# A graph network layer on one core: one-hot of the sums moved within the step, loads moved between queues, bias rows made on ScalarE

## The chip, the core and the metric

The kernel runs on one core of a Trainium2 chip. Time is device time in microseconds (us) of one launch. Each kernel is run several times, and runs of two kernels are compared on the same chip. The core's engines work side by side, each through its own instruction order: TensorE (PE in the profile, its weight loads PEld), VectorE (DVE), ScalarE (ACT), GpSimd (POOL) and SyncE (SP, which here only issues transfers and reads addresses). An instruction waits for semaphores of other engines and of transfers; everything behind it on its engine waits too.

## The reference

A node has 128 features, there are N = 12500 nodes and E = 400000 edges, sorted by target (`dst`). Per edge a message is built from both ends' rows, scaled by an edge weight and by a small network over 32 edge features; scores go through a softmax over all edges of the same target; values are summed per target.

```python
h = jnp.maximum(_layernorm(x, axis=-1), 0.0)
message = (h @ w_src + b_src)[src] + (h @ w_dst)[dst]
message = message * edge_weight1 * _radial_mlp(edge_attr_32, ...)
message = message @ w_sep + b_sep
msg_h = message.reshape(n_edges, H, AH + VH)
alpha = _smooth_leaky_relu(msg_h[:, :, :AH])
value = msg_h[:, :, AH:]
score = jnp.einsum('ehk,ahk->eh', alpha, alpha_dot)
att = _segment_softmax(score, dst, n_nodes)[..., None]
out = jax.ops.segment_sum(value * att, dst, num_segments=n_nodes)
x = x + out.reshape(n_nodes, H * VH) @ w_proj + b_proj
```

Everything is float32; H = 8 heads with 16 + 16 channels.

## The kernel before

All stages are written in an order fixed by hand: within a stage the program's order is each engine's order. Tiles come from pools with a fixed number of buffers, and a tile that is made anew waits until the readers of its older buffer are done.

**The node stage** (lines 154 to 342) makes two tables in device memory, `t_src` and `t_dst`, from layer norm, relu and two products. It goes over 98 tiles of 128 nodes in 25 quads of 4 tiles. `stats` (DVE) and `norm` (ACT) run ahead, `turn` transposes a quad on PE and copies it on DVE, `products(i)` multiplies, copies to `ms` (4 buffers, mostly by ACT) and has SP store `ms` to the two tables. SP's queue holds, in this order: the 8 loads of x (L162, L163); the targets as `cur` and, shifted by one edge, as `prev`, both 125 rows of 3200 words (L169 to L172); the first target of each section, `base` (L176, two times 400 single words); the sections' ends, `ends` (L177, 1600 single words); 14 loads of weights in block form (L188 to L194); and then the table stores. ACT's queue starts with two loads and 15 more through `load` (L110). `fits()` after quad 12 checks that the targets are sorted and every section spans less than 64 targets. `cuts()` after the last quad turns `prev` and `cur` into marks (`sm`), stored to `same` for the softmax, and makes small constants (`w_s`, `v_out`, `b_s`, `far`, `tgt`).

**The step loop** (`windows`, L656 to L1181) does 400 steps, each for 1000 edges in two sections of 500. `step(k)` carries several steps at once: POOL's gathers of source rows for k+4 and k+5 (8 indirect transfers per step, L739), the edge network for k+1 to k+3, the message and scores of k, and for c = k - 12 the values times softmax weights (`values`, into `pvx`) and their sum per target (`sums`, L912: a product of `pvx` with a one-hot `oh` of each edge's place in its window of 64 targets). Every 8 steps the softmax of 16 sections runs: a scan forward (L852), a scan backward and a subtraction (L857, L862), an exponential on ACT and a transposition. In every eighth step from step 47 on, 25 times, `add_x` adds the output bias to a block of x that `load_x` fetched two steps before.

DVE's order in a regular step is: the one-hot's two instructions (L888, L891), `rad` twice, `mT` twice, `pvx` of section 0, `mr`, `al` of section 0, `pvx` of section 1, `al` of section 1, `ohT`, `m`, and behind these a scan where one is due. PE's order is `p3`, the sources' transposition, the message, V of section 0, pa, the network's first layer, V of section 1, sources, pa, second layer, `sums`, a transposition and, in odd steps, the scores.

After the last k 14 more steps empty the pipeline, with jobs between them that combine the windows' edges (L1144 to L1181).

**The last stage** (L1213 to L1289) divides the sums by the weights' total (`quotients`, 12 tiles at a time), transposes (`turn`), multiplies by `w_proj` and adds x and the value bias. Its loads are `g` (SP, 12 tiles each, 9 of them, three ahead) and `x_fin` (ACT's queue, 8 loads). Per tile DVE adds `v_out` times a factor per node (`has`) to x (L1270), and per quad it adds the product (L1274); SP stores the output.

Of the kernel before, what the change touches and what calls it, by code (L numbers as in the profile page):

```python
# [56 lines left out]
def gnn_kernel(ctx: ExitStack, tc: tile.TileContext, a: dict, out: bass.AP):  # L57
# [47 lines left out]
    ident = const.tile([P, P], F32, name="ident")  # L105
    make_identity(nc, ident)

    def load(name, shape, ap=None, eng=None):
        t = const.tile(shape, F32, name="c_" + name)
        (eng or nc.scalar).dma_start(out=t, in_=a[name] if ap is None else ap)  # L110
        return t

    eps = const.tile([P, 1], F32, name="eps")
    nc.vector.memset(eps, LN_EPS)
    ones = const.tile([P, P], F32, name="ones")
# [38 lines left out]
    with tc.tile_pool(name="node", bufs=2) as np_, tc.tile_pool(name="node1", bufs=1) as n1, \  # L154
# [6 lines left out]
        for t0, t1 in groups:  # L161
            nc.sync.dma_start(out=x_all[:, t0:t1, :], in_=x_v[:, t0:t1, :])  # L162
        nc.sync.dma_start(out=x_all[:tail, NF, :], in_=x[NF * P:, :])  # L163
        dst_r = dst.rearrange("(p c) -> p c", p=RP)
        cur = n1.tile([RP, RC], I32, name="cur")
        prev = n1.tile([RP, RC], I32, name="prev")
        ends = n1.tile([100, 8, 2], I32, name="ends")
        eb = n1.tile([P, NS, 2], I32, name="eb")
        nc.sync.dma_start(out=cur, in_=dst_r)  # L169
        nc.vector.memset(prev[0:1, 0:1], -1)  # L170
        nc.sync.dma_start(out=prev[0:1, 1:RC], in_=dst_r[0:1, 0:RC - 1])
        nc.sync.dma_start(out=prev[1:RP, :], in_=dst[RC - 1:E - 1].rearrange("(p c) -> p c", c=RC))  # L172
        at = dst[0:1]
        with nc.allow_non_contiguous_dma(reason="the sections' ends"):
            for f in range(2):
                nc.sync.dma_start(out=base[:, f, :], in_=dst_h[f:f + 1, :, 0])  # L176
            nc.sync.dma_start(out=ends, in_=bass.AP(  # L177
                at.tensor, at.offset, [[8 * SEC, 100], [SEC, 8], [SEC - 1, 2]]))

        w1b = const.tile([P, P], F32, name="w1b")  # L180
        nc.vector.memset(w1b, 0.0)
        w2b = const.tile([P, P], F32, name="w2b")
        w3b = const.tile([P, C], F32, name="w3b")
        b12 = const.tile([P, 2], F32, name="b12")
        for f in range(2):
            for q in range(2):
                o = (2 * q + f) * RAD
                nc.sync.dma_start(out=w1b[o:o + RAD, f * FC:(f + 1) * FC], in_=a["fc_w1"])  # L188
            s = slice(f * FC, (f + 1) * FC)
            for q in range(2):  # L190
                nc.sync.dma_start(out=w2b[s, q * FC:(q + 1) * FC], in_=a["fc_w2"])
            nc.sync.dma_start(out=w3b[s, :], in_=a["fc_w3"])
            nc.sync.dma_start(out=b12[s, 0:1], in_=a["fc_b1"])
            nc.sync.dma_start(out=b12[s, 1:2], in_=a["fc_b2"])  # L194
        b_n = load("b_n", [C, 1], a["b_src"].rearrange("o c -> c o"))
        dot = load("dot", [C, 1])
        heads = load("heads", [C, C])
        w1, b1 = load("fc_w1", [RAD, FC]), load("fc_b1", [FC, 1])
        w2, b2 = load("fc_w2", [FC, FC]), load("fc_b2", [FC, 1])
        w3, b3 = load("fc_w3", [FC, C]), load("fc_b3", [C, 1])  # L200
        w_a, b_a = load("w_a", [C, C]), load("b_a", [C, 1])
        w_v = load("w_v", [C, C])
        w_proj = load("w_proj", [C, C])
        b_out = load("b_out", [P, C], a["b_proj"].to_broadcast([P, C]))
        b_v = load("b_v", [C, 1])


        mv = n1.tile([P, NB, 2], F32, name="mv")
# [60 lines left out]


        def fits():
            gt = n1.tile([RP, RC], BF16, name="gt")
            nc.vector.tensor_tensor(gt, prev, cur, op=ALU.is_gt)
            cnt = n1.tile([P, 2], F32, name="cnt")
            nc.vector.memset(cnt, 0.0)
            nc.vector.tensor_reduce(cnt[:RP, 0:1], gt, AX.X, ALU.add)
            span = n1.tile([100, 8], F32, name="span")
            nc.vector.tensor_sub(span, ends[:, :, 1], ends[:, :, 0])
            nc.vector.tensor_scalar(span, span, float(W - 1), None, op0=ALU.is_ge)
            nc.vector.tensor_reduce(cnt[:100, 1:2], span, AX.X, ALU.add)  # L280
            tot = nps.tile([1, 1], F32, name="tot", bufs=1)
            for j in range(2):
                nc.tensor.matmul(tot, cnt[:, j:j + 1], ones[:, 0:1], start=(j == 0), stop=(j == 1))
            nc.vector.tensor_copy(bad, tot)
            nc.sync.dma_start(out=ends_d[:, 1:2 * NS + 1].rearrange("o (p c) -> (o p) c", p=100),
                              in_=ends.rearrange("p s i -> p (s i)"))
            none = n1.tile([1, 2], I32, name="none")
            nc.vector.memset(none, -1)
# [12 lines left out]
        v_out = const.tile([P, C], F32, name="v_out")  # L301

        def cuts():
            sm = n1.tile([RP, RC], BF16, name="sm")
            nc.vector.tensor_tensor(sm, prev, cur, op=ALU.not_equal)
            nc.vector.tensor_scalar(sm, sm, RESTART, None, op0=ALU.mult)
            nc.sync.dma_start(out=same[:, 0:E].rearrange("o (p c) -> (o p) c", p=RP), in_=sm)
# [24 lines left out]
        for i in range(Q):  # L332
            if i % 2 == 0 and 4 * i + G < NB:
                stats(4 * i + G, min(4 * i + 2 * G, NB))
            if i + 2 < Q:
                norm(i + 2)
            if i + 1 < Q:
                turn(i + 1)
            products(i)
            if i == 12:  # L340
                fits()
        cuts()


    chunks = [(t, min(CH, TPI - t)) for t in range(0, TPI, CH)]
# [310 lines left out]
    def windows():  # L656
# [5 lines left out]
        with tc.tile_pool(name="wk2", bufs=2) as sp, tc.tile_pool(name="ps", bufs=1, space=PSUM) as pp, \  # L662
# [214 lines left out]
                nc.scalar.copy(Pem[m].rearrange("p t q h -> p t (q h)"), pt)  # L877


            def sums_begin(c):  # L880
                pvx[c] = sp.tile([T, 2, TS, ROW], F32, name="pvx")
                q = c % MP * 2
                for f in range(2):
                    nc.scalar.copy(pvx[c][:, f, :, C:ROW], Pem[c // MP][:, :, q + f, :])
                _, loc = prep[c // 16]
                ohs[c] = sp.tile([T, 8, W], F32, name="oh")
                t0 = c % 16 * 8
# [60 lines left out]
            def step(k):  # L948
# [28 lines left out]
                if has(k + 1):  # L977
                    split_md(k + 1, 0)
                if has(c):
                    sums_begin(c)  # L980
                rad = mlp3(k) if has(k) else None
                if has(k):
                    sources(k, 1)
# [13 lines left out]
                    mlp1(k + 2)  # L997
                if has(c):
                    values(c, 1)

                if has(k + 1):
                    sources(k + 1, 0)
# [210 lines left out]
    with tc.tile_pool(name="fin", bufs=3) as fp, tc.tile_pool(name="fin1", bufs=1) as f1, \  # L1213
# [4 lines left out]
        for t0, t1 in groups:  # L1218
            nc.scalar.dma_start(out=x_all[:, t0:t1, :], in_=xb_v[:, t0:t1, :])
        nc.scalar.dma_start(out=x_all[:tail, NF, :], in_=xb[NF * P:N, :])  # L1220
        gs, qs, qTs, has = {}, {}, {}, {}
        XQ = 12
        starts = list(range(0, NB, XQ))
# [35 lines left out]

        def finish(i):  # L1260
            t0, t1 = quads[i]
            qT = qTs.pop(i)
            py = fps.tile([P, 4, C], F32, name="py")
            for t in range(t0, t1):
                n = rows(t)
                nc.tensor.matmul(py[:n, t - t0, :], qT[:, t - t0, :n], w_proj, start=True, stop=True)
            for t in range(t0, t1):
                n, u = rows(t), t % XQ
                xt = x_all[:n, t, :]
                nc.vector.scalar_tensor_tensor(xt, v_out[:n], has[t0 // XQ][:n, u:u + 1], xt,  # L1270
                                               op0=ALU.mult, op1=ALU.add)
            for n, u0, u1 in blocks(t0, t1):
                y = x_all[:n, u0:u1, :]
                nc.vector.tensor_add(y, py[:n, u0 - t0:u1 - t0, :], y)  # L1274
                nc.sync.dma_start(out=out_v[:, u0:u1, :] if n == P else out[NF * P:N, :].unsqueeze(1), in_=y)

        NG = len(starts)
        for i in range(3):
            load_g(i)
        quotients(0)  # L1280
        turn(0)
# [44 lines left out]
```

## Time and profile before

| what | value |
|---|---|
| median of 3 runs | 4723.23 us (4720.04 to 4723.61) |
| the profiled execution: its time | 4712.63 us |
| its span | 4710.8 us |
| mean granted TensorE clock | 0.964 |
| node stage, to the first load of the step stage | 155.0 us |
| POOL's first gather | 160.28 us |
| first load of the last stage | 4626.5 us |

Busy over the whole span, and the two stages at the ends as 40 slices show them (one digit is a slice of 117.8 us in tenths of busy time; PEclk is the granted clock):

```profile
PE 4212.0 (89%) x29692; PEld 2344.1 (50%) x29692; DVE 3081.2 (65%) x6005; ACT 1921.9 (41%) x4595; POOL 3136.0 (67%) x3223
...
PE   4669998999999999999999999999999999999974
...
PEclk8779999999999999999999999999999999999987
```

A line of the profile's tables reads: line of the kernel, engine, operation, output <- inputs, shapes, count, busy time and mean of one, then the engine's idle time just before and what ended most of it. In a timeline the first two numbers are start and duration in us. A wait list reads: who waited for whom, total us, how often, longest. An engine's share over the whole span is a mean over stages with different limits, so the stages are read on their own.

### The profile page before, as it was taken

The numbers are of one execution on the slowest core, as the hardware profiler recorded it, in microseconds if no ns is written. First come the engines' busy times: TensorE is split into PE (matmuls) and PEld (weight loads), VectorE is DVE, ScalarE is ACT, GpSimd is POOL, SyncE is SP. The second block draws the span as 40 slices with busy tenths as digits, with TensorE's granted clock in tenths as the row PEclk, the third lists the DMA queues.
The fourth block names the chain that finished last, engine by engine and source line by source line (L and its number), as shares of the span: only waits on it lengthen the run. The fifth ranks groups of instructions, "written<-read, shape, count | busy, mean of one in ns | idle before, by whom it ended". The sixth has DMA issues, their size and how long they took to land.

```text
span 4710.8 us, 88096 instructions
## 1 busy us (share of the span) xinstructions
PE 4212.0 (89%) x29692; PEld 2344.1 (50%) x29692; DVE 3081.2 (65%) x6005; ACT 1921.9 (41%) x4595; POOL 3136.0 (67%) x3223
## 2 busy tenths in 40 slices
PE   4669998999999999999999999999999999999974
PEld 3325554554555555555545555555555555555553
DVE  4436665766766666666666666666666666666666
ACT  3324443443443444443433444444444444444421
POOL 0467776776777777777766777777777767777601
PEclk8779999999999999999999999999999999999987
DMA  4667767777776777777777777777677777777724
GB/s 160 168 162 173 175 167 172 174 178 175 170 176 171 169 176 175 172 178 174 170 175 170 177 174 169 179 172 164 171 174 169 171 168 170 172 168 174 173 64 173
DMA packets 901312, 796.36 MB, mean 169 GB/s; under 512 B 530125, under 2 KB 776829, under 8 KB 900598
## 3 DMA queue, kind: packets, MB, share of 16 engines
q1 hardware_dynamic: 794830, 573.36, 46.8%
q0 software_dynamic: 102816, 210.37, 21.5%
q10 hardware_dynamic: 3202, 6.92, 0.4%
q8 instruction: 234, 3.83, 0.4%
q14 instruction: 230, 1.88, 0.1%
HBM read 649.99 MB, written 140.67 MB: 168 GB/s over the span
## 4 chain that ended last, share of the span: by engine, by line
PE 66%; DVE 10%; DMA 9%; SPq 6%; ACT 5%; issue 4%; POOL 1%; ACTq 0%; POOLq 0%; DVEq 0%
PE pa L820 14%; PE V L901 13%; PE misc L912 7%; PE p L790 6%; PE pm L803 6%; PE pm L811 4%; PE p L758 4%; PE misc L831 4%; PE p L773 4%; DMA md<-t_dst 2%; DMA sc_d<-Sp 2%; PE m L749 2%; ACT sl L822 2%; DMA agg<-ob 2%; DVE al L824 2%
## 5 line engine op out<-in xcount | busy, mean ns | idle before, releaser
L739 POOL DMA_INDIRECT gs<-t_src,idx x3200 | 3121.6, 976 | 1347.2 <-issue 800.8
L822 ACT ACTIVATE sl<-pa,c_b_a 128x500 f32<-128x500 f32 x800 | 541.4, 677 | 1595.5 <-PE pa L820 1594.7
L824 DVE SCALAR_TENSOR_TENSOR al<-pa,sl 128x500 f32<-128x500 f32 x800 | 543.1, 679 | 828.8 <-ACT sl L822 723.6
L820 PE MATMUL pa<-mT,c_w_a 128*128 128x500 f32 x1600 | 851.2, 614 | 244.2 <-DVE mT L816 173.3
L901 PE MATMUL V<-c_w_v,mT 128*125 128x128 f32 x6208 | 895.5, 288 | 0.3
L901 PEld LDWEIGHTS V<-c_w_v,mT 128*125 128x125 f32 x6208 | 746.4, 190 | 290.7 <-issue 176.8
L794 DVE SCALAR_TENSOR_TENSOR rad<-p,c_fc_b,w_b 128x500 f32<-128x500 f32 x800 | 552.9, 733 | 307.2 <-PE p L790 305.7
L903 DVE TENSOR_TENSOR pvx<-V,Pem 125x512 f32<-125x512 f32 x776 | 531.9, 685 | 114.4 <-PE V L901 107.8
L816 DVE SCALAR_TENSOR_TENSOR mT<-pm,c_b_n,rad 128x500 f32<-128x500 f32 x800 | 552.5, 733 | 6.5 <-PE pm L811 6.5
L803 PEld LDWEIGHTS pm<-ident,gs 125*128 125x128 f32 x3200 | 356.7, 142 | 312.8 <-issue 292.3
L803 PE MATMUL pm<-ident,gs 125*128 125x125 f32 x3200 | 505.0, 280 | 7.9 <-DMA gs<-t_src,idx 7.9
L912 PE MATMUL misc<-pvx,oh 125*64 125x136 f32 x6400 | 470.1, 288 | 31.4 <-DVE pvx L903 27.6
L912 PEld LDWEIGHTS misc<-pvx,oh 125*64 125x64 f32 x6400 | 364.5, 138 | 182.9 <-issue 178.6
L790 PE MATMUL p<-h,w3b 64*128 64x500 f32 x1600 | 446.0, 634 | 2.4 <-ACT h L776 2.4
L820 PEld LDWEIGHTS pa<-mT,c_w_a 128*128 128x128 f32 x1600 | 245.0, 193 | 284.5 <-DVE mT L816 195.4
L811 PE MATMUL pm<-ohT,m 64*128 64x500 bf16 x2400 | 323.9, 376 | 0.0
L758 PE MATMUL p<-eT,w1b 64*128 64x250 f32 x1600 | 287.5, 437 | 1.0 <-ACT eT L751 1.0
L725 ACT CAST m<-md 128x128 bf16<-128x128 f32 x400 | 118.3, 296 | 401.1 <-DMA md<-t_dst 400.8
L758 PEld LDWEIGHTS p<-eT,w1b 64*128 64x128 f32 x1600 | 124.7, 191 | 307.5 <-issue 276.3
L761 ACT ACTIVATE h<-p,b 128x500 f32<-128x500 f32 x400 | 272.4, 681 | 4.8 <-PE p L758 4.8
L776 ACT ACTIVATE h<-p,b 128x500 f32<-128x500 f32 x400 | 269.2, 673 | 3.6 <-PE p L773 3.6
L888 DVE TENSOR_TENSOR oh<-lane,loc 125x504 f32<-125x504 f32 x400 | 269.2, 673 | 0.0
(145 smaller groups left out, 3286.1 us busy)
## 6 DMA issues: line engine op xcount, KB each, us to landing
w_b<-in_edge_weight SPq DMA_DIRECT2D x400, 500.0 KB
d_b<-in_dst SPq DMA_DIRECT2D x400, 250.0 KB
gs<-t_src,idx POOLq DMA_INDIRECT x3200
e_t<-in_edge_attr SPq DMA_DIRECT2D x400, 125.0 KB
sc_d<-Sp SPq DMA_DIRECT2D x200, 250.0 KB
win<-ob SPq DMA_DIRECT2D x400, 68.0 KB
agg<-ob SPq DMA_DIRECT2D x800, 33.5 KB
md<-t_dst SPq DMA_DIRECT2D x800, 32.0 KB
```

What stands on the lines that cost most here:

```text
L739: nc.gpsimd.indirect_dma_start(out=gs[:, j, :], out_offset=None, in_=t_src[:, :], in_offset=bass.IndirectOffsetOnAxis(ap=idx[:, t:t + 1], ...
L758: nc.tensor.matmul(p1[:, q, 0:2 * T], w1b[s, :], eTs[k][s, :], start=True, stop=True)
L790: nc.tensor.matmul(p3[:, f, 0:SEC], w3b[s, :], h2s[k][s, :], start=True, stop=True)
L794: nc.vector.scalar_tensor_tensor(rad[:, s], p3[:, f, 0:SEC], b3, w_g[k][:, s], op0=ALU.add, op1=ALU.mult)
L803: nc.tensor.matmul(pms[k, f][:, t * T:(t + 1) * T], gs[:T, t, :], ident[:T, :T], start=(t == 0), stop=False, is_transpose=True, skip_group ...
L816: nc.vector.scalar_tensor_tensor(mTs[k][:, s], pm[f], b_n, rad[:, s], op0=ALU.add, op1=ALU.mult)
L820: nc.tensor.matmul(pa, w_a, mTs[k][:, f * SEC:(f + 1) * SEC], start=True, stop=True)
L822: nc.scalar.activation(sl, pa, AF.Silu, bias=b_a, scale=1.0)
L824: nc.vector.scalar_tensor_tensor(al, pa, 0.25, sl, op0=ALU.mult, op1=ALU.add)
L901: nc.tensor.matmul(V[:, t, :], mTs[c][:, o:o + T], w_v, start=True, stop=True)
L903: nc.vector.tensor_mul(pvx[c][:, f, :, 0:C].rearrange("p t (h k) -> p t h k", h=H), V.rearrange("p t (h k) -> p t h k", h=H), Pem[c // MP] ...
L912: nc.tensor.matmul(acc[f * W:(f + 1) * W, :], ohs[c][:, f * TS + t, :], pvx[c][:, f, t, :], start=(t == 0), stop=(t == TS - 1), skip_group ...
```

## The change

Four edits.

1. The one-hot of the sums: `sums_begin` is split. Its copies stay where they were (`weights`), its two DVE instructions (`one_hot`) are called after `values(c, 1)`, that is behind the second `pvx` and ahead of the second `al`. In the steps after the last k, too, they follow the two `pvx`.
2. Targets: one tile `cur` of 128 rows with 3126 words takes the place of `cur` and `prev`: 3125 words per row by one load, and the word before them by a second load of 127 single words. `fits` and `cuts` compare the tile with itself shifted by one. The marks leave as 128 rows of 3125.
3. Loads: the targets' loads and all weights (15 that were on ACT's queue, 14 that were on SP's) go to SP's queue behind the table stores of quads 0 and 1. `cuts` is called after quad 20 instead of after the last.
4. The last stage: x is loaded through SP's queue, behind the first load of `g` and ahead of the second. `v_out` times `has` is made by ACT into a new tile `vh`, four instructions per quad; GpSimd adds `vh` to x, one instruction per quad (two for the last); DVE adds the product.

```diff
+        def load_targets():
+            nc.sync.dma_start(out=cur[:, 1:CC + 1], in_=dst.rearrange("(p c) -> p c", p=P))
+            at = dst[CC - 1:CC]
...
+                nc.sync.dma_start(out=cur[1:P, 0:1], in_=bass.AP(at.tensor, at.offset, [[CC, P - 1], [1, 1]]))
...
+            if i == 1:
+                load_targets()
+                load_weights()
             if i == 12:
                 fits()
-        cuts()
+            if i == 20:
+                cuts()
...
-            def sums_begin(c):
+            def weights(c):
                 pvx[c] = sp.tile([T, 2, TS, ROW], F32, name="pvx")
...
+            def one_hot(c):
                 _, loc = prep[c // 16]
...
                 if has(c):
-                    sums_begin(c)
+                    weights(c)
...
                 if has(c):
                     values(c, 1)
+                    one_hot(c)
...
+        def load_x():
+            for t0, t1 in groups:
+                nc.sync.dma_start(out=x_all[:, t0:t1, :], in_=xb_v[:, t0:t1, :])
...
         def finish(i):
             t0, t1 = quads[i]
+            vh = fp.tile([P, 4, C], F32, name="vh")
+            for t in range(t0, t1):
+                n, u = rows(t), t % XQ
+                nc.scalar.activation(vh[:n, t - t0, :], v_out[:n], AF.Identity, scale=has[t0 // XQ][:n, u:u + 1])
+            for n, u0, u1 in blocks(t0, t1):
+                y = x_all[:n, u0:u1, :]
+                nc.gpsimd.tensor_tensor(y, y, vh[:n, u0 - t0:u1 - t0, :], op=ALU.add)
...
-                nc.vector.scalar_tensor_tensor(xt, v_out[:n], has[t0 // XQ][:n, u:u + 1], xt,
-                                               op0=ALU.mult, op1=ALU.add)
...
         NG = len(starts)
-        for i in range(3):
+        load_g(0)
+        load_x()
+        for i in range(1, 3):
             load_g(i)
```

More of the change, by code (lines that the diff above doesn't have):

```diff
@@ L106, in gnn_kernel @@
     make_identity(nc, ident)
[L108 to L111, printed above, removed]
     eps = const.tile([P, 1], F32, name="eps")
@@ L163, in gnn_kernel @@
         nc.sync.dma_start(out=x_all[:tail, NF, :], in_=x[NF * P:, :])
[L164 to L178, printed above, removed]
         w1b = const.tile([P, P], F32, name="w1b")
@@ L184, in gnn_kernel @@
         b12 = const.tile([P, 2], F32, name="b12")
[L185 to L204, printed above, removed]
@@ L205, in gnn_kernel @@
-        b_v = load("b_v", [C, 1])
+        CC = E // P
+        cur = n1.tile([P, CC + 1], I32, name="cur")
+        nc.vector.memset(cur[0:1, 0:1], -1)
+        ends = n1.tile([100, 8, 2], I32, name="ends")
+        eb = n1.tile([P, NS, 2], I32, name="eb")
+        wt = {name: const.tile(shape, F32, name="c_" + name) for name, shape in (
+            ("b_src", [C, 1]), ("dot", [C, 1]), ("heads", [C, C]), ("fc_w1", [RAD, FC]), ("fc_b1", [FC, 1]),
+            ("fc_w2", [FC, FC]), ("fc_b2", [FC, 1]), ("fc_w3", [FC, C]), ("fc_b3", [C, 1]), ("w_a", [C, C]),
+            ("b_a", [C, 1]), ("w_v", [C, C]), ("w_proj", [C, C]), ("b_proj", [P, C]), ("b_v", [C, 1]))}
@@ new lines, in gnn_kernel @@
+        b_n, dot, heads, w1, b1, w2, b2, w3, b3, w_a, b_a, w_v, w_proj, b_out, b_v = wt.values()
+        def load_targets():
+            nc.sync.dma_start(out=cur[:, 1:CC + 1], in_=dst.rearrange("(p c) -> p c", p=P))
+            at = dst[CC - 1:CC]
+            with nc.allow_non_contiguous_dma(reason="single targets"):
+                nc.sync.dma_start(out=cur[1:P, 0:1], in_=bass.AP(at.tensor, at.offset, [[CC, P - 1], [1, 1]]))
+                for f in range(2):
+                    nc.sync.dma_start(out=base[:, f, :], in_=dst_h[f:f + 1, :, 0])
+                at = dst[0:1]
+                nc.sync.dma_start(out=ends, in_=bass.AP(
+                    at.tensor, at.offset, [[8 * SEC, 100], [SEC, 8], [SEC - 1, 2]]))
@@ new lines, in load_weights @@
+        def load_weights():
+            for name, t in wt.items():
+                ap = a[name]
+                if name == "b_src":
+                    ap = ap.rearrange("o c -> c o")
+                elif name == "b_proj":
+                    ap = ap.to_broadcast([P, C])
+                nc.sync.dma_start(out=t, in_=ap)
+            for f in range(2):
+                for q in range(2):
+                    o = (2 * q + f) * RAD
+                    nc.sync.dma_start(out=w1b[o:o + RAD, f * FC:(f + 1) * FC], in_=a["fc_w1"])
+                s = slice(f * FC, (f + 1) * FC)
+                for q in range(2):
+                    nc.sync.dma_start(out=w2b[s, q * FC:(q + 1) * FC], in_=a["fc_w2"])
+                nc.sync.dma_start(out=w3b[s, :], in_=a["fc_w3"])
+                nc.sync.dma_start(out=b12[s, 0:1], in_=a["fc_b1"])
+                nc.sync.dma_start(out=b12[s, 1:2], in_=a["fc_b2"])
@@ L271, in fits @@
         def fits():
-            gt = n1.tile([RP, RC], BF16, name="gt")
-            nc.vector.tensor_tensor(gt, prev, cur, op=ALU.is_gt)
+            gt = n1.tile([P, CC], BF16, name="gt")
+            nc.vector.tensor_tensor(gt, cur[:, 0:CC], cur[:, 1:CC + 1], op=ALU.is_gt)
             cnt = n1.tile([P, 2], F32, name="cnt")
             nc.vector.memset(cnt, 0.0)
-            nc.vector.tensor_reduce(cnt[:RP, 0:1], gt, AX.X, ALU.add)
+            nc.vector.tensor_reduce(cnt[:, 0:1], gt, AX.X, ALU.add)
             span = n1.tile([100, 8], F32, name="span")
@@ L303, in cuts @@
         def cuts():
-            sm = n1.tile([RP, RC], BF16, name="sm")
-            nc.vector.tensor_tensor(sm, prev, cur, op=ALU.not_equal)
+            sm = n1.tile([P, CC], BF16, name="sm")
+            nc.vector.tensor_tensor(sm, cur[:, 0:CC], cur[:, 1:CC + 1], op=ALU.not_equal)
             nc.vector.tensor_scalar(sm, sm, RESTART, None, op0=ALU.mult)
-            nc.sync.dma_start(out=same[:, 0:E].rearrange("o (p c) -> (o p) c", p=RP), in_=sm)
+            nc.sync.dma_start(out=same[:, 0:E].rearrange("o (p c) -> (o p) c", p=P), in_=sm)
             nc.sync.dma_start(out=same[:, E:E + 1], in_=sm[0:1, 0:1])
@@ L1217, in gnn_kernel @@
         out_v = out[0:NF * P, :].rearrange("(p t) c -> p t c", t=NF)
-        for t0, t1 in groups:
-            nc.scalar.dma_start(out=x_all[:, t0:t1, :], in_=xb_v[:, t0:t1, :])
-        nc.scalar.dma_start(out=x_all[:tail, NF, :], in_=xb[NF * P:N, :])
+        def load_x():
+            for t0, t1 in groups:
+                nc.sync.dma_start(out=x_all[:, t0:t1, :], in_=xb_v[:, t0:t1, :])
+            nc.sync.dma_start(out=x_all[:tail, NF, :], in_=xb[NF * P:N, :])
         gs, qs, qTs, has = {}, {}, {}, {}
@@ L1266, in finish @@
                 nc.tensor.matmul(py[:n, t - t0, :], qT[:, t - t0, :n], w_proj, start=True, stop=True)
-            for t in range(t0, t1):
-                n, u = rows(t), t % XQ
-                xt = x_all[:n, t, :]
-                nc.vector.scalar_tensor_tensor(xt, v_out[:n], has[t0 // XQ][:n, u:u + 1], xt,
-                                               op0=ALU.mult, op1=ALU.add)
             for n, u0, u1 in blocks(t0, t1):
```

## The prediction

> **What bounds it now.** First the table of busy time in stretches of the span, then the strip of the page and the list of waits. Columns: stretch, its length, PE, weight loads, DVE, ACT, POOL busy (instructions), granted clock, DMA share, GB/s.
>
> ```profile
> 50.00:100.00 50.00, 20.78 (x84) 14.57 (x84) 19.88 (x83) 20.00 (x49) 0.00 (x0) 0.72 0.40 143
> ...
> 800.00:1200.00 400.00, 372.67 (x2667) 205.30 (x2665) 269.80 (x517) 166.26 (x403) 289.93 (x295) 0.98 0.72 175
> ...
> 4650.00:4711.00 61.00, 33.63 (x234) 32.09 (x233) 54.84 (x141) 11.10 (x20) 0.00 (x0) 0.88 0.49 171
> ```
>
> Three stages, three limits. In the first no engine is half busy. In the step loop PE is busy 93%. In the last DVE is busy 54.8 of 61 us. What PE still waits for in the loop (360 to 4480 us; total, times, longest):
>
> ```profile
> PE pa L820 <- DVE mT L816: 153.0, 81, 9.7
> PE pa L820 <- DVE al L824: 46.6, 63, 2.6
> ```
>
> **Part 1, the one-hot (L888, L891).** A regular step, in the timeline:
>
> ```profile
> 2062.58 0.69 DVE L903 TENSOR_TENSOR pvx<-V,Pem 125x512 f32<-125x512 f32 x1 [0.30 <-PE V L901]
> ...
> 2064.33 0.89 PEld L912 LDWEIGHTS misc<-pvx,oh 125*64 125x64 f32 x16 [0.37 <-issue]
> ...
> 2064.63 0.68 DVE L824 SCALAR_TENSOR_TENSOR al<-pa,sl 128x500 f32<-128x500 f32 x1 [1.35 <-ACT sl L822]
> ```
>
> The new place is the 1.35 us hole between the second pvx and the second al. Its user, the sums (L912), begins 1.06 us after that pvx ends. The pair takes 0.67 us of DVE's order (below, from the start of oh, 2067.63, to that of rad, 2068.30), and the short second half ends 0.09 us later: about 0.70 after pvx. So a regular step keeps some 0.35 us of cover: cost nothing. Without that cover, each 0.1 us of lateness is 0.1 x 388 steps = 39 us on PE.
>
> The gain is where DVE is late at a step's start. After the backward scan, once in 8 steps:
>
> ```profile
> 2065.81 1.19 DVE L857 TENSOR_TENSOR_SCAN M<-sm,M 128x500 f32<-128x500 bf16 x1
> ...
> 2067.04 0.68 DVE L862 TENSOR_TENSOR M<-S,M 128x500 f32<-128x500 f32 x1
> ...
> 2067.63 0.68 DVE L888 TENSOR_TENSOR oh<-lane,loc 125x504 f32<-125x504 f32 x1
> ...
> 2068.30 1.38 DVE L794 SCALAR_TENSOR_TENSOR rad<-p,c_fc_b,w_b 128x500 f32<-128x500 f32 x2
> ...
> 2070.38 1.11 PE L820 MATMUL pa<-mT,c_w_a 128*128 128x500 f32 x2 [1.11 <-DVE mT L816]
> ```
>
> scan, subtraction, one-hot, rad, mT, pa: PE waits 1.11 us, of which 0.67 is the one-hot. 48 such steps: 32 us. The remaining 0.44 stays, and so does the wait on al (0.70 us in the same step: it follows pa through a table load of 1.28 us and sl). Late there next is pvx, which follows al; the one-hot behind it ends 0.35 us before the sums need it, as above. Likewise rad stands behind the one-hot where DVE waited for xs (L938 on its DMA: 74.9 us, 17 times): 17 x 0.67 = 11 us; and behind the forward scan (L852), where PE's timeline has some 15 waits between 0.2 and 3.0 us: about 8. Sum 52 us at most. But xs comes through SP, which runs about a step late (load_x is step 5's and was issued at 2019.77, in step 7). In those 17 groups of 8 PE may arrive earlier only to wait longer: 17/48 of 32 = 11 off. I take **-41** (ends -15 and -55).
>
> In the 12 steps after the last k the one-hot now hides under V (L901); behind pvx it stands before the sums: 0.67 x 12 = 8 at most. From 4531 us on DVE works off scans and a 9.75 us reciprocal, and order among its own work is free; about 4 steps pay: **+3** (0 to +8).
>
> **Part 2, the loads.** SP's queue, and the DMA share in 40 slices of 15 to 75 us:
>
> ```profile
> 32.95 13.82 SPq L177 DMA_DIRECT2D ends<-in_dst  x1
> 46.89 15.71 SPq L188 DMA_DIRECT2D w1b<-in_fc_w  x2
> ...
> 70.05 0.52 SPq L266 DMA_DIRECT2D t_src<-ms  x1
> ```
> ```profile
> DMA  7999999423334332322223522221111101011699
> ```
>
> The first table store leaves at 70.05 although ms was ready by 28: SP is stuck in loads. The share of 3 tenths for so long is the point. The Trainium skill, "DMA: Bandwidth & Descriptors", section "Why a DMA increments its semaphore by 16 and not by 1", says that a transfer runs on the largest number of engines up to 16 that divides its slowest dimension: 125 rows give 5, 128 give 16, 127 give 1. 5/16 is 0.31: the trace agrees. cur and prev (125 x 12.8 KB each) crawl on 5 engines, and the single words of ends and base queue behind them. The row alone (13.82 us for ends) would let the new block keep its length; by the rule cur as 128 x 3125 takes about 1.6 MB / 400 GB/s = 4 us, prev is gone, and what stays is issue time. The rule also speaks against the 127-word column, but its words are few.
>
> New order on SP: x, the stores of quads 0 and 1, targets, 15 + 14 weights, then the other stores. ACT's first activation was at 14.53, behind its 17 loads, while its statistics were ready at 7.8: it starts some 7.9 us earlier, so quad 1's ms is done at 28.1 - 7.9 = 20.2. Then two stores 0.9, cur 0.3, column 0.6 (row rb, L680: 0.64), base 2 x 2.52 (the first L176 issue), ends 4 x 2.52 = 10.1, 15 weights 8.3 (ACT's rows, 0.33 to 1.01 each), 14 weights 7.8: resumed at about 53 instead of 70.05: -17. If every wait in SP's old rows came back (8 + 4 + 15), at 80. At the resumption two more quads are stored: -6.3 (quads 6 to 8, 81.28 to 87.61). cuts moves into the stream at quad 20: 7.6 us of DVE (3.48, 0.99, 0.98, 1.14 and small ones); fits, 6.9 us of DVE, stretched two stores to 11.7 us against 3.2; so +8, less 3.6 because three quads behind it find their inputs ready: +4.5. The tail goes: the last store ended at 146.96, but the next stage waited for the marks:
>
> ```profile
> 147.07 7.77 DMA same<-sm
> ```
>
> So next loads at 147 - 17 - 6.3 + 4.5 + 2 for landing = 130 instead of 155.0: **-25** (ends -31 and +1).
>
> **Part 3, the last stage.** DVE per 3 quads: quotients 2.88, 12 x L1270 (1.13 per 4), 3 x L1274: 8.32 us by the repeat of L1241 (4643.24, 4651.56). L1270 leaves: 4.9. ACT gains 12 activations of 128x128 with a scale per row; nearest row is L231 (0.41 us apart), so 12 x 0.41 + 3 x 0.55 = **6.6**, the new pace; with the plain cast (L725, 0.30) DVE's 4.9 would set it. POOL adds 128x512 three times: its rows here are a memset (680 elements, 0.65 us: 0.49) and an affine select (128 elements, 0.28: 1.1 for four). The skill's "GPSIMD Engine Reference", section 3.1, speaks against the move: a two-input add is about twice VectorE's time, 4497 ns for 2048 elements, so an estimate of 1.1 to 1.2 us here. By either it is under 3.6 of 6.6 us: hidden; it would decide only above 2.2 each. No run here shows it yet. Against it goes the load order: x (6.4 MB) now stands ahead of g(1) on one queue and arrives at about 4628.5 + 8.05 MB / 0.415 = 4648, while quotients(1) ran at 4643.24. From quad 3 (4651) 22 quads x 2.2 = 48, then add, add and store 4.5 (DVE's last op to the end took 2.9): 4704 instead of 4710.8: **-7** (ends -18 and +5).
>
> **Sum**: -41 + 3 - 25 - 7 = -70 us against this execution's 4712.6 (span 4710.8). The runs' median is 4723.2, 10.6 above it; the difference is set on the median: **4653 us**.
>
> **Rivals.** (a) The loop doesn't pay: SP or POOL paces it. POOL's 64 gathers in 8 steps take 64 x 1.245 = 79.7 us, and 8 steps without xs take 82.3; so POOL has 2.6 us left, more than 0.67. SP's lateness speaks for it. Then -25 + 3 - 7 = -29: 4694. (b) The first block keeps its length, the words being slow in themselves: start 0, time 4678. (c) **Slower**: the sums wait for the one-hot in every step. Place: L912 behind the L891 of its own step; 0.35 us of cover. For it: one semaphore is now fresh where it was 9 us old. It eats the 70 us from 0.18 us per step, i.e. if the pair takes 0.53 us longer than its 0.67; at 0.25 us it is 388 x 0.25 - 70 = +27: 4750. Against it: L888 shows 673 ns as a mean over 400, and its neighbours would not change. (d) GpSimd's adds at 3 us each: 25 x 3 = 75 us pace the last stage, +15 there: 4675. That the change doesn't act is excluded: DVE's order does move.
>
> **Numbers.** Forecast 0.58 (own range 4625 to 4680), a 0.17, b 0.12, c 0.07, d 0.06. The range 4615 to 4700 takes in a, b and d. 0.2% (9.4 us) is about what a measurement can tell from no change: faster 0.89, same 0.04 (a with b), slower 0.07 (c).
>
> **What shows it.** Part 1: PE's wait on mT after the backward scan 0.44 instead of 1.11, DVE's hole before al about 0.65, no wait before L912. Part 2: the third quad's store near 53, the first load of the step stage near 130, a DMA share without a long 3. Part 3: L1241's repeat at 6.6 us, its second start near 4648 less the shift. Wrong if L912 names a wait on oh, or if PE's busy share in the loop stays at 93%.

## The result, and the profile after

| | before | after |
|---|---|---|
| median of 6 runs | 4722.19 us (4716.71 to 4730.83) | 4700.86 us (4693.17 to 4705.99) |
| ratio, 95% interval | | 0.9956 (0.9943 to 0.9969) |
| profiled execution, its span | 4710.8 us | 4702.7 us |
| node stage, to the first load of the step stage | 155.0 | 121.5 |
| from there to the first `rad` | 18.2 | 18.1 |
| step loop, first to last `rad` | 4331.9 | 4336.8 |
| last `rad` to the first load of the last stage | 121.5 | 121.3 |
| last stage, first load to the end | 84.2 | 105.0 |

Forecast: 4653 us, with an own range of 4625 to 4680. It is faster, by 21 us of the 70. The start gave 33.5 us, the last stage took 20.8 back, and the loop, from which 41 were to come, gave nothing. (The stages are those of one profiled execution each and add up to the 8.1 us between the two spans; the medians differ by 21, so a loop gain of up to some 13 us can't be excluded.) Most of the experiments below met a step loop of some 14 us a step instead of 10.7 (the kernel before then takes 6030 to 6183 us), with the two outer stages about as long as here. So a time is compared only with that of the kernel before measured beside it, and a stage by its own length.

Busy time by stretches, as before (length, PE, weight loads, DVE, ACT, POOL, clock, DMA share, GB/s):

```profile
50.00:100.00 50.00, 35.27 (x151) 26.81 (x151) 34.80 (x122) 33.26 (x82) 0.00 (x0) 0.85 0.46 172
800.00:1200.00 400.00, 377.60 (x2699) 208.62 (x2696) 270.25 (x513) 170.81 (x413) 288.10 (x297) 0.98 0.73 173
4642.00:4703.00 61.00, 33.93 (x194) 32.48 (x194) 27.91 (x46) 28.48 (x82) 21.88 (x19) 0.73 0.33 115
```

At the start PE is busy 35 us of 50 instead of 21. In the last stage DVE has fallen from 54.8 to 27.9 us of 61, and yet the stage is longer: nothing is full any more, so a chain of waits sets the pace.

**Loop.** The step after the backward scan did what was promised. Timeline after:

```profile
2035.38 1.19 DVE L861 TENSOR_TENSOR_SCAN M<-sm,M 128x500 f32<-128x500 bf16 x1
2036.61 0.68 DVE L866 TENSOR_TENSOR M<-S,M 128x500 f32<-128x500 f32 x1
2037.20 1.38 DVE L798 SCALAR_TENSOR_TENSOR rad<-p,c_fc_b,w_b 128x500 f32<-128x500 f32 x2
2038.50 1.37 DVE L820 SCALAR_TENSOR_TENSOR mT<-pm,c_b_src,rad 128x500 f32<-128x500 f32 x2
...
2039.28 1.11 PE L824 MATMUL pa<-mT,c_w_a 128*128 128x500 f32 x2 [0.45 <-DVE mT L820]
```

No one-hot between subtraction and `rad`; PE waits 0.45 us instead of 1.11. Over steps 40 to 398 the interval from one `rad` to the next is, as a mean by place in the group of 8, 10.85 -> 10.19 us in step 3, but 11.36 -> 11.69 in step 7 and 11.68 -> 11.88 in step 0. In the steps with xs (40 to 240) a group of 8 takes 87.24 -> 87.25 us, without xs (240 to 392) 85.18 -> 85.09. So what is gained is given back within the group, and not at xs alone. (A step's interval is the one that ends with its `rad`.) Who waits more is in the waits of the loop (after, 326 to 4450 us; then before, 360 to 4480):

```profile
ACT m L729 <- DMA md<-t_dst: 407.3, 137, 6.7
...
PEld misc L918 <- DVE oh L897: 138.3, 369, 0.4
PE pa L824 <- DVE mT L820: 135.2, 86, 9.0
...
DVE xs L944 <- DMA xs<-in_x: 103.8, 22, 9.7
```
```profile
ACT m L725 <- DMA md<-t_dst: 321.4, 120, 7.1
...
DVE xs L938 <- DMA xs<-in_x: 74.9, 17, 9.7
```

PE's wait on mT fell by 18 us only, while ScalarE waits 86 us longer for `md`, the targets' rows, which SP loads three steps ahead, and VectorE 29 us longer for xs. Both of the prediction's signs of being wrong came. The weight load of the sums now names `oh`, in 369 places; that cost little, 0.4 us at the longest, and before there stood waits of the same size without a releaser ("issue": 143.6 us in 382). And PE's busy share in the loop stayed: 3859 of 4120 us before, 3872 of 4124 after, 94% both.

**SP in the loop**, timeline of the kernel after (copy of a step's sums, load of `md`, cast of `md`, store of those sums):

```profile
3255.52 0.27 ACT L922 COPY ob<-misc 128x136 f32<-128x136 f32 x1 [0.38 <-PE misc L918]
...
3265.80 1.25 SPq L723 DMA_DIRECT2D md<-t_dst  x2
...
3270.08 0.30 ACT L729 CAST m<-md 128x128 bf16<-128x128 f32 x1 [3.14 <-DMA md<-t_dst]
...
3271.58 0.34 SPq L926 DMA_DIRECT2D win<-ob  x1
```

Here `md` is issued 3 us before it is used, not three steps (as medians over 40 steps 3.1 to 5.9 us from step 240 on and 8.2 to 9.9 from 40 to 240; 20 or more in the kernels below that run at 14 us a step). And the store of sums copied at 3255.5 leaves at 3271.6: SP is a step and a half behind. As means over 40 windows each (the last over 28), from the end of the copy to the store's issue, SP is 15.0 to 17.3 us late from window 240 on (before the change 13.2 to 16.6), and 8.8 to 10.2 us from 40 to 240, while xs is in the loop (7.4 to 9.2).

**Start.** SP's rows and the DMA share in 40 slices of 15 to 75 us:

```profile
28.01 0.92 SPq L185 DMA_DIRECT2D ends<-in_dst  x1
...
46.48 0.51 SPq L266 DMA_DIRECT2D t_src<-ms  x1
...
121.48 0.34 SPq L678 DMA_DIRECT2D ri<-in_src  x1
```
```profile
DMA  9992998722921123210113999991746009360720
```

`ends` holds SP 0.92 us instead of 13.82, and quad 2's store leaves at 46.5 instead of 72.1 (the first store of all at 17.3 instead of 70). The long run of threes is gone.

**Last stage**, one group of 12 tiles:

```profile
4653.35 1.75 DVE L1254 TENSOR_TENSOR q<-g,r 128x1536 f32<-128x1536 f32 x1
...
4655.24 0.63 PE L1265 MATMUL pt<-ident,q 128*128 128x128 f32 x4 [4.20 <-DVE q L1254]
...
4655.96 0.59 ACT L1268 COPY qT<-pt 128x512 f32<-128x512 f32 x1 [3.97 <-PE pt L1265]
4656.44 1.28 ACT L1275 ACTIVATE vh<-v_out,has 128x128 f32<-128x128 f32 x4
...
4657.80 1.28 POOL L1278 TENSOR_TENSOR x_fin<-x_fin,vh 128x512 f32<-128x512 f32 x1 [4.41 <-ACT vh L1275]
...
4659.11 0.69 DVE L1286 TENSOR_TENSOR x_fin<-py,x_fin 128x512 f32<-128x512 f32 x1 [3.42 <-POOL x_fin L1278]
```

A bracket names the row above it: q, transposes, qT, the rows vh behind it on ScalarE, GpSimd's add, VectorE's add; and the next quotients stand behind the group's last such add. The quotients repeat every 9.7 to 11.4 us (8.3 to 8.7 before), and the second group starts 16.8 us after the first instead of 9.5, because its `g` stands behind x.

### The profile page after: what moved, and what is told of

Same layout as the page of the kernel before. It is cut to its first block, busy times and chain, and to the rows that moved or that the text cites. A ratio compares the mean times of both kernels' runs of the same rounds, so it can differ in the third digit from the quotient of the medians.

```text
span 4702.7 us, 88132 instructions
## 1 busy us (share of the span) xinstructions
PE 4221.4 (90%) x29692; PEld 2354.5 (50%) x29692; DVE 3058.6 (65%) x5907; ACT 1947.9 (41%) x4693; POOL 3151.6 (67%) x3249
## 5 line engine op out<-in xcount | busy, mean ns | idle before, releaser
L820 DVE SCALAR_TENSOR_TENSOR mT<-pm,c_b_src,rad 128x500 f32<-128x500 f32 x800 | 552.6, 732 | 8.0 <-PE pm L815 8.0
L807 PE MATMUL pm<-ident,gs 125*128 125x125 f32 x3200 | 505.2, 280 | 10.1 <-DMA gs<-t_src,idx 9.9
L918 PE MATMUL misc<-pvx,oh 125*64 125x136 f32 x6400 | 463.5, 287 | 38.2 <-DVE oh L897 38.2
## 6 DMA issues: line engine op xcount, KB each, us to landing
agg<-ob SPq DMA_DIRECT2D x800, 33.5 KB
```

What stands on the lines that cost most here:

```text
L807: nc.tensor.matmul(pms[k, f][:, t * T:(t + 1) * T], gs[:T, t, :], ident[:T, :T], start=(t == 0), stop=False, is_transpose=True, skip_group ...
L820: nc.vector.scalar_tensor_tensor(mTs[k][:, s], pm[f], b_n, rad[:, s], op0=ALU.add, op1=ALU.mult)
L918: nc.tensor.matmul(acc[f * W:(f + 1) * W, :], ohs[c][:, f * TS + t, :], pvx[c][:, f, t, :], start=(t == 0), stop=(t == TS - 1), skip_group ...
```

## The experiments

### The parts alone

One-hot alone (`sums_begin` split, nothing else), the new start alone, the new last stage alone (each on the kernel before), and the change without its last stage:

> The kernel before with the one-hot in its new place and nothing else. Theory A (the loop gives back what the one-hot gains while VectorE waits for xs, whose load is issued only about a step ahead of its use): the time does not move, 4722 +- 8 us; after the backward scan PE's wait on mT shortens by about 0.66 us, and the waits of VectorE on the load of xs grow from 75 us to about 100. Theory B (the loop of the changed kernel is held back by something that the new loads at the start or the new last stage cause): the one-hot alone is worth its predicted 41 us, 4681.

> The kernel before with the first stage of the changed kernel (targets and weights behind the stores of the second quad, 128-row targets, marks in mid-stream); one-hot and last stage as before. If the parts add, as the shift of the first load of the step stage says (121.5 us instead of 155.0), 33 us less: 4689. If the loop eats part of it because the transfers of the start reach into it, 4695 to 4705.

> The kernel before with the last stage of the changed kernel and nothing else. By the traces (first load of that stage to the end: 84.2 us before, 105.0 after) 20 us more than before. The forecast had 7 less. A rival (the last stage is only slow because the loop and start of the changed kernel shifted something, such as the last rows' store) has about 0.

> The changed kernel with the last stage of before. If the parts add: 21 us less than the changed kernel, about 38 to 45 less than before. If the one-hot's parts only pay on some chips, the ratio to before here is that of the two parts run alone, multiplied.

| kernel | ratio to before (95%) | loop, first to last `rad` | its stage |
|---|---|---|---|
| one-hot alone | 0.985 (0.9817 to 0.9883) | 5540 | |
| start alone | 0.9919 (0.989 to 0.9948) | 5672 | first load of the steps at 122.8 |
| last stage alone | 1.0051 (1.0014 to 1.0087) | 5801 | 103.7 us |
| change without last stage | 0.9501 (0.9471 to 0.9532) | 5501 | 122.2; 83.9 us |

Start and last stage carry their whole effect by themselves: the first load of the steps at 122.8 us against 155.6 to 160.0 in the kernels with the old start, and 103.7 us of last stage against the 83.7 to 87.3 of the kernels with the old one. But the one-hot, worth nothing in the result, gains 1.5% here, where the loop takes 14 us a step. Neither theory A nor B had expected that. The first two kernels of the table were measured beside one before (6057.9 us), the last two beside another (6168.4). The change without its last stage gains more than the product of its two parts (0.977); why is open.

### The loads of xs (theory A)

```diff
-                if 0 <= i < Q and q == 5:
+                if 0 <= i < Q and q == 3:
                     load_x(i)
```

on the kernel before, and with the one-hot moved as well; both were run again, and once in the whole change without its last stage ("best").

> The kernel before with the load of xs issued two steps earlier (in step 3 of 8 instead of step 5) and nothing else. Theory A: VectorE's waits on that load go from 75 us in 17 quads to under 15, and as what stands behind xs in VectorE's order are rad and mT, PE gets most of it: 30 to 55 us less, 4667 to 4692. Rival A2 (the place of SP in its queue, or another transfer, holds the loop at the same pace whatever VectorE waits for): within 10 us of 4722.

> The kernel before with both: the one-hot in its new place, and the load of xs two steps earlier. Theory A: with the cover of xs gone the one-hot pays what the scan steps promise, 48 x 0.66 = 32 us below the kernel with the early load alone, about 4635 to 4660. Rival A2, or a rival A3 (PE itself is the pace, and a shorter wait on mT is refilled by its other waits): no more than 10 us below the kernel with the early load alone.

> Repeat on another chip of the kernel before with xs loaded two steps earlier alone. At 10.7 us a step: VectorE's waits on that load from 75 us to under 15, time 4667 to 4692 by theory A, 4712 to 4732 by rival A2. At 14 us a step: no change, as PE is late for everything.

> Repeat on another chip of the kernel before with the one-hot moved and xs loaded two steps earlier. If this chip runs the step loop at some 10.7 us a step (4722 us in all before), theory A expects 4635 to 4660; rival A3 (PE refills it) less than 10 us below the kernel with the early load alone. If it runs the loop at 14 us a step, as the two chips of the last runs, 1.5 to 2.5% less than before.

> The changed kernel with the last stage of before and xs loaded two steps earlier. At 10.7 us a step: the start's 33 us, the one-hot's 32 and what the earlier xs frees (30 to 55) without the last stage's 21 us: 4600 to 4640. If A2 or A3 holds: 4675 to 4690. At 14 us a step: 4.5 to 6% less than before.

> The kernel before with the one-hot moved and xs loaded two steps earlier, again on another chip, because the three chips of the last runs ran the step loop at some 14 us a step (over 6050 us in all before) and the result was measured at 10.7 us a step. If this chip runs it at 10.7: theory A 4635 to 4660, A2 or A3 (nothing gained in the loop, whatever xs does) 4710 to 4722. At 14 us a step: 1.5 to 3.5% less than before, as on the other chips.

Early xs alone: 0.9975 (0.9943 to 1.0006) and 1.0019 (0.9983 to 1.0056), nothing. With the one-hot: 0.9809 (0.9772 to 0.9846), 0.9677 (0.9635 to 0.9719) and 0.9872 (0.9776 to 0.9967), no better than the one-hot alone. "Best": 0.9607 (0.9564 to 0.9649). All six ran at 14 us a step, where VectorE does not wait for xs, so they can't decide A at 10.7. What speaks against A as the whole cause is the trace after itself: the groups without xs gained nothing either.

In place of A came theory S: **SP's queue paces the loop** at 10.7 us a step. There SP is behind by 15 us; at 14 us it has time to spare, its store comes 2.1 to 2.5 us after the copy, and a shorter way on VectorE is worth something. What SP's own queue waits for tells the two apart, 400 to 4400 us, after and then one-hot alone:

```profile
SPq L930 <- DMA agg<-ob: 128.1, 215, 2.0
SPq L845 <- DMA sc_d<-Sp: 120.7, 45, 3.9
SPq L706 <- PE pm L807: 18.8, 43, 0.6
```
```profile
SPq L836 <- ACT m L725: 613.0, 119, 10.0
SPq L870 <- DVE M L857: 89.0, 31, 7.1
```

In the kernel after, SP waits for engines in 147 of 4000 us, never longer than 1.3 us; another 252 us it waits for transfers, most of them its own earlier stores. At 14 us a step it waits for engines in 953 of 4000 us, up to 10.0 us at a time. Same rows as in the timeline above, the one-hot alone in its second measurement, at 14 us a step:

```profile
3259.43 0.27 ACT L918 COPY ob<-misc 128x136 f32<-128x136 f32 x1 [0.33 <-PE m L749]
3260.43 0.30 ACT L725 CAST m<-md 128x128 bf16<-128x128 f32 x1
...
3260.93 0.34 SPq L922 DMA_DIRECT2D win<-ob  x1
```

The cast of `md` has no bracket: it waits for nothing; the store leaves 1.2 us after the copy.

### SP made the pace on purpose (theory S)

If S holds, loading SP with useless work until it paces must make the one-hot's gain vanish. 16 loads of one word per step, into tiles nobody reads:

```diff
+            def burden():
+                for _ in range(16):
+                    t = lp.tile([1, 1], I32, name="spare", bufs=32)
+                    nc.sync.dma_start(out=t, in_=dst[0:1].rearrange("(o c) -> o c", o=1))
...
                 if has(k + 3):
+                    burden()
                     load_w(k + 3)
```

> The kernel before with the one-hot moved and nothing else, as the control for the two loaded kernels of this call. Theory S (SP's queue paces the step loop at 10.7 us a step; where a chip runs the loop slower for another reason, SP is idle a third of the time and VectorE's order counts again): on a chip at 14 us a step 1.5 to 3% less than before; on a chip at 10.7 us a step within 0.3% of before.

> The kernel before with 16 more loads of one word on SP's queue in every step, into tiles that nobody reads. At 0.35 us an issue they take 5.6 us of SP per step beside the 10.3 it has: 16 us a step, so that SP paces the loop on any chip: about 6500 us (6300 to 6900), its store of the sums issued 10 us or more after the sums are copied, instead of 2.2 us.

> The same 16 loads a step, and the one-hot moved. Theory S: where SP paces, the move is worth nothing, within 0.4% of the kernel with the loads alone (as +5 us in the loop of the changed kernel). Its rival (the move pays by what it takes from VectorE's path wherever VectorE is late, and the result's loop lost it to something else): the 1.5 to 3% below the kernel with the loads alone that the move is worth without them on this chip.

Measured side by side, with before at 6182.63 us:

| kernel | median | loop | store after the copy, from window 240 |
|---|---|---|---|
| one-hot alone | 5905.7 us, 0.9542 (0.9498 to 0.9587) | 5529 | 2.1 to 2.4 us |
| 16 loads | 6539.29 us (6534.03 to 6548.31) | 6136 | 20.5 to 23.6 us |
| 16 loads and one-hot | 6517.95 us (6508.67 to 6524.32) | 6120 | 21.4 to 25.3 us |

277 us of gain without the loads (4.6%, more than the 1.5 to 3% expected), 21 us (0.33%) with them: inside the 0.4% that S had set. From window 40 to 240 the stores come 7 to 14 us after the copy with the 16 loads, and 18 to 19 with the one-hot moved too. The waits of the loop show the same exchange as in the result; 400 to 4400 us, 16 loads without, then with the one-hot moved:

```profile
ACT m L730 <- DMA md<-t_dst: 108.5, 38, 9.3
...
DVE xs L943 <- DMA xs<-in_x: 60.4, 14, 10.0
```
```profile
ACT m L730 <- DMA md<-t_dst: 469.4, 107, 10.5
...
DVE xs L945 <- DMA xs<-in_x: 250.3, 25, 15.5
```

What VectorE no longer needs reappears as waits on SP's loads. The steps shift alike, too: without xs 15.6 -> 14.9 us in step 2 and 19.0 -> 16.1 in step 6, but 12.95 -> 14.4 in step 3; the group of 8 stays at 120.7 -> 120.6 us. The 16 loads follow each other every 0.295 us (median), 4.7 us a step; 120.6 / 8 - 4.7 = 10.4 us is an estimate of what SP needs for the rest, its waits for earlier stores included, against the 10.6 us a step of the result's loop (85.09 / 8).

So where SP has no time to spare, the move is worth next to nothing, and in the result's loop it had next to none. PE stands close behind, and the profile's chain for before, which follows who released whom, runs through PE for 66% of the span and through SP's queue for 6%. But PE is not the pace alone: in before, its busy time is 81.1 us of a group of 87.2 with xs and 80.4 of 85.2 without. With 0.7 us more to do on PE, the group with xs is 2 us longer. PE would leave some 0.6 to 0.8 us a step to a loop freed of SP, an estimate from these busy times.

### Less on SP

The change without its last stage, with `w_b`'s load and the windows' store on ScalarE's queue:

```diff
-                nc.sync.dma_start(out=w_g[k], in_=ew_p[:, k, :].to_broadcast([P, PR]))
+                nc.scalar.dma_start(out=w_g[k], in_=ew_p[:, k, :].to_broadcast([P, PR]))
...
-                nc.sync.dma_start(out=win[c * P:(c + 1) * P, :], in_=accs[c])
+                nc.scalar.dma_start(out=win[c * P:(c + 1) * P, :], in_=accs[c])
```

> The one-hot moved, the start of the changed kernel, the last stage of before, and the loads of w_b and the stores of the windows' sums taken from SP's queue to ScalarE's (about 1 us less of SP per step). Theory S: on a chip at 10.7 us a step the loop becomes 0.5 to 1 us a step shorter, 4300 to 4520 in all; on a chip at 14 us a step, where SP waits anyway, no less than the kernel without this relief (4 to 5% below before), since ScalarE only gets more to do.

0.974 (0.9685 to 0.9795), loop 5691 us, at 14 us a step: no gain there, rather a loss against the 5529 us of the one-hot alone beside it. S had expected no gain at this pace; what it forecast for 10.7, a shorter loop, no run has met, and it stays open.

### The start: order or layout

The changed kernel with the targets in 125 rows (tile, marks and word column; order as changed):

```diff
-        CC = E // P
-        cur = n1.tile([P, CC + 1], I32, name="cur")
+        CC = E // RP
+        cur = n1.tile([RP, CC + 1], I32, name="cur")
```

> The changed kernel with the targets in 125 rows of 3200 words instead of 128 of 3125; order of the loads, one fetch instead of two and the marks' place as changed. The forecast's reading (the layout sets how many of the 16 engines carry the transfer, and the block behind it waits for that): the share of DMA stays near 3 tenths for some 12 us, the 1.6 MB land about 8 us later, the single words of base and ends behind them too, the third quad's store leaves at 53 to 58 us instead of 46.5, and the first load of the step stage at 126 to 133 instead of 121.5. The rival (with the order changed the targets are hidden behind the weights' issue and the other quads' work, the order alone made the gain): third store within 2 us of 46.5, first load within 2 us of 121.5.

Quad 2's store at 53.57 instead of 46.48, the first load of the steps at 128.5 instead of 121.5, and the threes are back (slices of 15 to 75 us, and SP's first weight):

```profile
DMA  9993833335433332201421101169999917630366
```
```profile
28.82 9.03 SPq L195 DMA_DIRECT2D c_b_src<-in_b_src  x1
```

SP is held 9.03 us at the first weight (1.30 with 128 rows); that the targets' transfer holds it there is the reading, which the threes of the same microseconds support. The other kernels with the new start had their first load at 121.5 to 123.2. So some 5 to 7 of the 33.5 us are the layout, and the rest is the order with the single fetch and the marks' place, which were not separated.

### The last stage: chain or order of loads

Three edits of the changed kernel: the rows and GpSimd's add one quad ahead; x on ScalarE's queue; both.

```diff
-        def finish(i):
+        def ahead(i):
...
             if i + 1 < Q:
                 turn(i + 1)
+                ahead(i + 1)
             finish(i)
```
```diff
-                nc.sync.dma_start(out=x_all[:, t0:t1, :], in_=xb_v[:, t0:t1, :])
+                nc.scalar.dma_start(out=x_all[:, t0:t1, :], in_=xb_v[:, t0:t1, :])
```

> The changed kernel with ScalarE's rows and GpSimd's add of each quad made one quad ahead, behind the turn of the same quad. Theory C (the pace of the last stage is a chain: quotients, transposes, copy of qT, rows behind it on ScalarE, GpSimd's add, VectorE's add, and only then the next quotients): the repeat of the quotients goes from 10.4 us per 12 tiles to 7.0 to 7.6, and the stage from 105 us to about 80. Rival D (VectorE and GpSimd hold each other up at the memory's port, or ScalarE is full): the repeat stays within 0.7 us of 10.4.

> The changed kernel with the loads of x in the last stage back on ScalarE's queue, as before the change, so that the second group of sums doesn't wait behind 6.4 MB of x. The second quotients come 9 to 10 us after the first instead of 16.8, and the stage is about 7 us shorter, with the repeat still at 10.4 us. If the stage is held by the arrival of x instead, no change.

> The changed kernel with both edits of its last stage: x on ScalarE's queue, and the rows and GpSimd's add one quad ahead. If the two add (105.0 to 100.7 by the first, to 95.7 by the second), 91 us from the first load to the end, second quotients 10 us after the first and a repeat of 8.8 to 9.8 us: still longer than the 84 us with VectorE's multiply-and-add, so that the form itself costs. If it falls to 84 or below, the whole loss was order.

| kernel | last stage | second quotients after the first | repeat, mean of the next 7 |
|---|---|---|---|
| before | 84.2 us | 9.5 us | 8.4 us |
| after | 105.0 | 16.8 | 10.4 |
| rows ahead | 95.7 | 16.9 | 9.2 |
| x on ACT | 100.7 | 10.4 | 10.1 |
| both | 90.0 | 9.9 | 9.1 |

Rows ahead: theory C had the direction, not the size: 9.3 us less and a repeat of 9.2, not 25 and 7.0 to 7.6; rival D's repeat, within 0.7 us of 10.4, did not come either. The order of the loads: 4.3 us instead of 7. Both together came to 90.0 as their sum said (91.4), so 5.8 us stay that neither explains. These are single profiles; the form of before took 83.7 to 87.3 us in thirteen other kernels, and that of after 103.7 and 108.3 in two, so a difference of some 4 us is at the edge of what they tell. Both, parts of two groups:

```profile
4569.71 1.75 DVE L1254 TENSOR_TENSOR q<-g,r 128x1536 f32<-128x1536 f32 x1
4570.14 2.46 POOL L1278 TENSOR_TENSOR x_fin<-x_fin,vh 128x512 f32<-128x512 f32 x1 [0.38 <-ACT vh L1275]
...
4575.81 1.26 POOL L1278 TENSOR_TENSOR x_fin<-x_fin,vh 128x512 f32<-128x512 f32 x1 [0.38 <-ACT vh L1275]
4576.08 1.06 DVE L1251 TENSOR_SCALAR r<-g 128x96 f32<-128x96 f32 x1
```

Beside the quotients GpSimd's add takes 2.46 us instead of 1.26, and beside an add VectorE's row L1251 takes 1.06 us instead of 0.20 (its duration in seven of the eight full groups of the kernel after). That agrees with the lock which the Trainium skill, "SBUF — State Buffer", section "SBUF: two separate sides", describes: GpSimd shares a port pair with VectorE's instructions of certain forms, those with two inputs in SBUF among them, and whichever starts first holds it for the whole instruction while the other is blocked. In the changed kernel the chain kept the two apart but for one row L1251 (1.07 us); as soon as it is loosened they meet: five of GpSimd's adds take 2.45 to 2.83 us, and five of VectorE's rows L1251 0.84 to 1.07. How much of the 5.8 us this is was not measured by itself.

This last kernel also met the faster loop: 4613.62 us in its one run, against 4634.08 in the one run of before beside it. Taken with the stages of the earlier profile of before, its last stage costs 5.8 and its start gains 31.8 (123.2 against 155.0), and so what is left of the 20.5, the loop with the moved one-hot, shows no gain again (an estimate of 5.5 us more, smaller than the 14 us by which runs of before differ); SP's store comes 14.6 to 16.5 us after the copy there from window 240 on.

## Why the prediction was wrong

| term | predicted | profiled executions |
|---|---|---|
| node stage | -25 | -33.5 |
| step loop | -41 | +4.9 |
| steps after the last k | +3 | -0.2 |
| last stage | -7 | +20.8 |

**The loop** failed at the sentence "In those 17 groups of 8 PE may arrive earlier only to wait longer: 17/48 of 32 = 11 off". SP was seen a step late, but charged to the xs groups alone, as if xs were the only thing that SP brings; the path through VectorE to PE was priced as if nothing else set the pace. SP brings `md`, `w_b`, `e_t` and `d_b` for every step; the wait that says so, ScalarE's 321 us on `md` in 120 places, was the largest wait on a transfer in the kernel before, and the prediction does not use it: beside PE's waits it takes only VectorE's on xs. In place of 41 us gained the loop took 4.9 longer: PE's wait on mT lost 18 us, those on `md` and xs grew by 86 and 29. Rival (a) had named SP and gave 4694 us, close to 4700.9 by luck: its sum has the last stage at -7 instead of +20.8. Right were the 0.67 us per scan step (1.11 -> 0.45), the regular step (the sums did not become late: rival (c) did not occur), and VectorE's hole before the second `al` (0.68 as a mean, predicted 0.65).

**The start** had its mechanism right, and a term too large: `ends` was priced at 4 x 2.52 = 10.1 us from rows of before, in which SP was held behind `cur` and `prev`; freed of them it took 0.92 (`base` took 6.46 instead of 5.04). That is most of why quad 2's store left at 46.5 instead of the predicted 53, and the first load at 121.5 instead of 130. The rule of the Trainium skill weighed there ("DMA: Bandwidth & Descriptors", section "Why a DMA increments its semaphore by 16 and not by 1": the number of engines of a transfer divides its slowest dimension) agrees with the runs: 125 rows bring back the share of 3 tenths and cost 5 to 7 us.

**The last stage** failed at "so 12 x 0.41 + 3 x 0.55 = 6.6, the new pace". The repeat was 10.4. The durations were near (vh 0.32 us apart instead of 0.41, GpSimd's add 1.27 against the estimate of 1.1 to 1.2 from the Trainium skill's "GPSIMD Engine Reference", section 3.1). But the pace was taken from the fullest engine, as if the others ran beside it, and at the end of a group the program's order puts them one behind the other: vh stands behind qT on ScalarE, and the next quotients behind VectorE's add, which waits for GpSimd's. Loosening that order and the loads' recovers 15.0 of the 20.8 us. The late `g` of the second group was foreseen, at some 5 us (4648 against 4643.24); it cost 7.3 in the start of that group and 4.3 at the end.

**The steps after the last k**: PE's waits before the sums there now name `oh` (38.2 us in 13) instead of `pvx` and its copies (31.3 in 14), 7 us more where at most 8 were forecast, but the part as a whole is as long as before (121.3 instead of 121.5 us).

The change without the new last stage has the lowest ratio met, 0.9501 (0.9471 to 0.9532) at 14 us a step. At 10.7 it was not run; 4700.9 - 20.8, an estimate from the stages, would be 4680.

## What to carry to other kernels

Before pricing a shorter way on a compute engine, look for the queue that is late in the steady state: compare when it issues a load or store with when it could have. A load planned three steps ahead that lands just in time, on a queue that itself waits for almost nothing but its own transfers, points to a queue that paces; here the gain on VectorE came back as waits on it. The busy share of an engine gives its pace only if the program's order lets the others run beside it; where work is moved to two more engines, write down the chain through them before dividing by the fullest one.

## What was not expected of the hardware

The same program runs its loop at 10.7 or at 14 us a step: before took 6157.85 and, some 90 minutes later on the same chip, 4634.08 us. Why is open. At 14 us a step the engines' waits often end in something that the profile doesn't know: ScalarE's `sl` waits 389.8 us in 100 places without a releaser (one-hot alone, 400 to 4400 us), before at 10.7 us a step in none. And the granted clock drops in some of PE's idle spells; its mean over these kernels is 0.87 to 0.90 instead of 0.96. Start alone, stretches of 4 us (PE first, clock third from the end):

```profile
3016.00:3020.00 4.00, 1.69 (x14) 1.04 (x10) 1.42 (x3) 0.53 (x4) 3.09 (x4) 1.00 0.64 191
3020.00:3024.00 4.00, 1.79 (x6) 0.60 (x6) 1.38 (x2) 0.00 (x0) 2.41 (x3) 0.84 0.89 188
3024.00:3028.00 4.00, 2.49 (x12) 2.50 (x13) 1.87 (x4) 1.56 (x3) 0.00 (x0) 0.50 0.54 128
```

PE is idle more than half of 8 us, and the granted clock falls to half; the same comes again at 3064 us. Before at 10.7 us a step showed 1.00 in every such stretch from 3000 to 3112 us. Whether the clock is a part of the cause or only follows the idle spells was not measured. What one edit is worth differs between the two paces: the one-hot's move gained 1.5% and 4.6% at 14 us a step, and nothing at 10.7.
